# A four-layer graph-attention kernel: one layer summed by VectorE, sums taken two steps later, neighbour places in pairs

## The chip, the cores and the metric

The kernel runs on one core of a Trainium2 chip. The metric is the device time of one execution in microseconds; the number for a version is the median of its runs. A separate profiled execution gives the page and the trace, and its own time stands beside its span below.

The engines are named as in the profile: PE is TensorE (PEld its weight loads), DVE is VectorE, ACT is ScalarE, POOL is GpSimd, SP is SyncE. A line such as L753 is a line of the kernel before.

## The reference

There are 4096 nodes with 256 features each, in fp32, and a symmetric adjacency matrix in which each node has about eight neighbours on average, and itself. Four layers follow each other. Each takes the layer norm and ReLU of the features, applies one form of graph attention, and adds the result to the features:

```
h = relu(layernorm(x));  x = x + layer_l(h, adj)        # l = 0..3

layer 0:  Wh = h @ W            4 heads; e = leaky(s_i + s_j); softmax over neighbours; out = elu(sum_j a_ij Wh_j)
layer 1:  Wh = h @ W            1 head;  e = leaky(s1_i + s2_j); softmax;               out = Wh_i + sum_j a_ij h_j
layer 2:  Wh_head = h @ W_head + b   4 heads; the same kind of scores;                  out = sum_j a_ij Wh_j
layer 3:  q, k, v = h @ Wq + bq, ... 4 heads; scores q_i.k_j / 8, masked;               out = sum_j a_ij v_j
```

## The kernel before

The matrix is first read and turned into a list of neighbours for each node, and the nodes are sorted by how many neighbours they have. The 4096 sorted nodes then make 32 blocks of 128, one node in each partition. A block has as many places as its largest node has neighbours: `CAPS` goes from 23 down to 3 and sums to 277; 15 of the 32 counts are even and 17 odd. Layer 0 treats up to six of the neighbours ahead, so that it fetches `max(CAPS - 6, 0)` places, 93 in all.

A place is one neighbour for each of the block's 128 nodes. It is fetched by an indirect DMA on POOL (`fetch`, L529) from the layer's table of rows in DRAM into one slot of a ring in SBUF. The ring has 64 slots in layer 1, 69 in layer 2 and 36 in layer 3, where a row holds a key and a value. `fill(i)`, called at the start of step i, issues the fetches of blocks up to four ahead, as long as slots are free. `ORDER` takes the blocks alternately from the large and the small end (0, 31, 1, 30, and so on).

Every layer runs the same loop of 32 steps, one block a step, and every engine gets its instructions in the order in which the program is written (`tc.manual_schedule()`); nothing reorders them. One step i does this, with b the block of the step, c the one before it and d the one before that:

1. `fill(i)`: fetches on POOL.
2. `first(c)`: the first part of `settle` (only layer 0 has work there, two ACT instructions at L767 and L768).
3. `scores(b)`: DVE forms the attention scores of all places (in layer 3 with the products of queries and keys at L680 and L683), and ACT takes the exponential (L697) into `p`, a tile in PSUM.
4. `second(d)`: the norm's last part, ACT's ReLU (L507), PE's transposes (L515), ACT's copy of them (L516) and PE's product with the next layer's weights (L522, by `times` from `advance`).
5. `weigh(b)`: DVE normalises `p` (L732 to L734), multiplies the block's own row by its share (L741) and up to eight places at a time by theirs (L749). PE adds them up: one matmul with the identity for the own row (L745) and one for each place (L753), into the PSUM tile `acc`. An fp32 matmul appears in the trace as two passes, each with its weight load.
6. `settle(c)` goes on: DVE adds the sums of the previous block to the features (L780; L777 and L778 in layer 0; L772 in layer 3, which writes the output) and starts the statistics of the next norm.
7. `third(d)`: the rest of `advance`. It takes the product out of PSUM and makes the row of the next layer's table: L793 to L796 for layer 1, L800 and L801 for layer 2, L807 to L822 for layer 3. Rows for layers 2 and 3 are stored by SP's queue; those for layer 1 and the output by an indirect DMA on POOL (`send`, L535), which stands in POOL's order behind the fetches already issued.

After the loop the last two blocks are pushed through the remaining parts. The first fetch of a layer needs the whole table, and therefore the last row that the layer before it stores. PSUM holds two tiles for `acc`, three for `turned` and `times`, two for `p` and one for layer 3's query `q`.

Of the kernel before, what the change touches and what calls it, by code (L numbers as in the profile page):

```python
# [9 lines left out]
F32 = mybir.dt.float32  # L10
# [9 lines left out]
P = 128  # L20
# [45 lines left out]
class Sparse:  # L66
# [246 lines left out]
    def first_table(self, pool, rows, r):  # L313
# [8 lines left out]
        for k in range(4):  # L322
            t = 4 * r + k
            h = pool.tile([P, D], F32, name=f"s_h_t{t}", tag="h", bufs=2)
            nc.scalar.activation(
                h, xl[:, k, :], AF.Relu, bias=rn[:, 4 + k : 5 + k], scale=rn[:, k : k + 1]
            )
            ps = self.times(self.turned(pool, h, f"t0_{t}"), self.we0, W, f"t0_{t}")
            nc.scalar.copy(rows[:, t, :], ps)
# [180 lines left out]
    def turned(self, pool, h, name):  # L510
# [3 lines left out]
        for c in range(KC):  # L514
            nc.tensor.transpose(pt[:, ts(c, P)], h[:, ts(c, P)], self.ident)  # L515
        nc.scalar.copy(ht, pt[:, : KC * P].rearrange("p (c r) -> p c r", c=KC))  # L516
        return ht

# [26 lines left out]
    def layers(self):  # L545
        tc, nc, nt = self.tc, self.nc, self.nt
        with ExitStack() as ctx:
            big = ctx.enter_context(tc.tile_pool(name="s_big", bufs=1))
            self.pool = ctx.enter_context(tc.tile_pool(name="s_main", bufs=2))
            self.pacc = ctx.enter_context(tc.tile_pool(name="s_pacc", bufs=2, space=PSUM))  # L550
            self.pp = ctx.enter_context(tc.tile_pool(name="s_pp", bufs=3, space=PSUM))
            self.pe = ctx.enter_context(tc.tile_pool(name="s_pe", bufs=3, space=PSUM))

# [18 lines left out]
    def layer(self, l):  # L572

        nc, nt, vs = self.nc, self.nt, {}
# [6 lines left out]
        def fill(i):  # L584
            nonlocal at
            while todo and nt - len(todo) <= i + AHEAD:
                j = todo[0]
                K = self.slots(l, j)
                s = (at if at + K <= slots else 0) if K else 0
                if any(s < e and b < s + K for b, e in held.values()) or (l == 3 and len(held) > 3):  # L590
                    return
# [7 lines left out]
                for k in range(K):  # L599
                    at_k = self.near[:, j, k0 + k : k0 + k + 1]  # L600
                    self.fetch(ring[:, s + k, :], self.tab[l], at_k)
                held[j] = (s, s + K)
                at = s + K if K else at

        acc, behind, rows = {}, {}, {}

        def first(c):
            behind[c] = self.settle(l, c, acc.pop(c), made)
            next(behind[c])

        def second(d):
            if l < 3:
                ht = self.turned(self.pool, next(behind.pop(d)), f"{l + 1}_{d}")
                rows[d] = self.advance(l + 1, d, ht, made)
                next(rows[d])

        def third(d):
            if l < 3:
                next(rows.pop(d), None)
            for send in made:  # L620
                self.send(*send)
            made.clear()

        for i in range(nt):
            fill(i)
            b, c, d = (ORDER[k] if k >= 0 else None for k in (i, i - 1, i - 2))
            if c is not None:
                first(c)
            g = ring[:, held[b][0] : held[b][1], :]
            p = self.scores(l, b, self.rows[b], g)  # L630
            if d is not None:
                second(d)
            acc[b] = self.weigh(l, b, vs.pop(b) if l == 3 else self.rows[b][:, 0:D], g, p)
            del held[b]
            if c is not None:
                next(behind[c])
            if d is not None:
                third(d)
        c, d = ORDER[-1], ORDER[-2]
        first(c)  # L640
        next(behind[c])
        second(d)
        second(c)
        third(d)
        third(c)

    def scores(self, l, b, mine, g):
# [25 lines left out]
        else:  # L673
            q = self.pe.tile([P, D], F32, name=f"s_q_{b}", tag="q", bufs=1)
            nc.scalar.copy(q, mine[:, 0:D])
# [19 lines left out]
        )  # L695
        p = self.pe.tile([P, TOPK, H], F32, name=f"s_p_{l}_{b}", tag="p", bufs=2)
        nc.scalar.activation(p[:, : K + 1, :].rearrange("p k h -> p (k h)"), ek, AF.Exp)  # L697
# [17 lines left out]
    def weigh(self, l, b, me, g, p):  # L715
# [8 lines left out]
        else:  # L724
# [12 lines left out]
            mine = p[:, K, :]  # L737
        acc = self.pacc.tile([P, IB], F32, tag="acc", name=f"s_acc_{l}_{b}")
        v0 = 0 if l < 3 else D
        mev = pool.tile([P, D], F32, name=f"s_me_{l}_{b}", tag="me", bufs=2)  # L740
        nc.vector.tensor_tensor(  # L741
            mev.rearrange("p (h d) -> p h d", h=H), me.rearrange("p (h d) -> p h d", h=H),
            mine.unsqueeze(2).to_broadcast([P, H, D // H]), ALU.mult,
        )
        nc.tensor.matmul(acc[:, :D], lhsT=self.ident, rhs=mev, start=True, stop=(K == 0))  # L745
        for k0 in range(0, K, AT_ONCE):
# [4 lines left out]
            )  # L751
            for k in range(m):
                nc.tensor.matmul(  # L753
                    acc[:, :D], lhsT=self.ident, rhs=g[:, k0 + k, v0 : v0 + D],
                    start=False, stop=(k0 + k == K - 1),
                )
        return acc[:, :D]

    def settle(self, l, b, acc, made):
# [10 lines left out]
        if l == 3:  # L770
            y = pool.tile([P, D], F32, name=f"s_out_{b}", tag="out", bufs=3)
            nc.vector.tensor_tensor(y, xt, acc, ALU.add)  # L772
            made.append((self.out, self.own(b), y))
            yield None
            return
# [3 lines left out]
        else:  # L779
            nc.vector.tensor_tensor(xt, xt, acc, ALU.add)  # L780
        into = self.rows[b][:, 0:D] if l == 0 else None
# [607 lines left out]
```

## Time and profile before

| | us |
|---|---|
| median of 3 runs | 2269.25 |
| lowest, highest run | 2267.81, 2284.88 |
| profiled execution, its own time | 2277.38 |
| its span | 2275.6 |
| mean granted TensorE clock | 0.75 of full |
| DVE busy | 1270.9 (56% of the span) |
| POOL busy | 1212.4 (53%) |
| PE busy | 1175.5 (52%) |
| ACT busy | 444.1 (20%) |

| stretch, from a layer's first fetch to the next one's | from, to (us) | us |
|---|---|---|
| lists and sort | 0 to 522.46 | 522.5 |
| layer 0 | 522.46 to 813.45 | 291.0 |
| layer 1 | 813.45 to 1282.35 | 468.9 |
| layer 2 | 1282.35 to 1784.63 | 502.3 |
| layer 3 | 1784.63 to the end | 491.0 |

In a group's line of the page the columns are: line, engine, operation, tile written and tiles read, shape, count; then busy time in us and mean ns of one; then the engine's idle time just before these instructions, and what ended most of it. In the timeline they are start, busy time, engine, line, operation, and in brackets the idle time ahead of it and what released it. "remote" stands there where no releaser was found among this core's recorded events.

### The profile page before, as it was taken

What the parts mean: (1) busy time and instruction counts of PE and PEld (TensorE: products, weight loads), DVE (VectorE), ACT (ScalarE), POOL (GpSimd) and SP (SyncE); (2) the same over time, 40 slices, a digit from 0 to 9 for tenths busy, and PEclk for the clock granted to TensorE, in tenths of its full rate; (3) what the DMA queues carried; (4) which work ended last, traced back from release to release, by engine and by line L of the source; (5) the groups of instructions that cost most, each with busy time, mean ns of one, the idle gap of its engine ahead of it and who ended that gap; (6) DMA issues with size and microseconds to landing.
All of it is one profiled execution on the core that took longest, in us unless ns stands there. A gap on an engine that the chain in (4) does not pass through costs nothing. (4 is left out here: it accounts for less than half of the span.)

```text
span 2275.6 us, 17106 instructions
## 1 busy us (share of the span) xinstructions
PE 1175.5 (52%) x3977; PEld 795.2 (35%) x3999; DVE 1270.9 (56%) x3688; ACT 444.1 (20%) x1320; POOL 1212.4 (53%) x1354
## 2 busy tenths in 40 slices
PE   4767677611466613454566333566668242445354
PEld 2434334301344402333445222344446131334233
DVE  7657787711466711444466313455569465667666
ACT  5754343000233300111111101112123100000000
POOL 1055666556455457566653375655660465666662
PEclk9887889855687855677788756778789665667777
DMA  8988885305233244333432243333331555666662
GB/s 271 297 288 308 300 259 178 88 13 108 75 99 102 76 88 114 93 104 106 111 104 73 57 110 86 102 100 93 109 107 45 145 171 156 182 181 184 179 180 66
DMA packets 128244, 313.24 MB, mean 138 GB/s; under 512 B 31844, under 2 KB 58983, under 8 KB 128136
## 3 DMA queue, kind: packets, MB, share of 16 engines
q0 software_dynamic: 69088, 207.53, 33.3%
q1 hardware_dynamic: 59048, 104.55, 13.6%
q8 instruction: 34, 0.56, 0.1%
q14 instruction: 74, 0.61, 0.1%
HBM read 276.91 MB, written 35.07 MB: 137 GB/s over the span
## 5 line engine op out<-in xcount | busy, mean ns | idle before, releaser
L529 POOL DMA_INDIRECT s_ring<-s_tab,s_near x924 | 878.0, 950 | 599.5 <-issue 239.8
L753 PE MATMUL s_acc<-s_ring,s_ident 128*128 128x256 f32 x1848 | 510.0, 434 | 80.8 <-issue 59.9
L753 PEld LDWEIGHTS s_acc<-s_ring,s_ident 128*128 128x128 f32 x1848 | 409.6, 224 | 179.1 <-issue 73.6
L745 PE MATMUL s_acc<-s_me,s_ident 128*128 128x256 f32 x256 | 107.7, 511 | 410.6 <-issue 135.3
L749 DVE TENSOR_TENSOR s_ring<-s_ring,s_p 128x256 f32<-128x256 f32 (+7 forms) x169 | 267.1, 1605 | 0.0
L529 POOL DMA_INDIRECT s_g<-s_tab,s_listrow x192 | 184.2, 960 | 113.0 <-issue 53.9
L301 DVE MAX8 s_cand<-s_pt 128x8 f32<-128x256 f32 x512 | 188.4, 419 | 81.6 <-remote 40.5
L745 PEld LDWEIGHTS s_acc<-s_me,s_ident 128*128 128x128 f32 x256 | 61.7, 253 | 436.0 <-issue 232.8
L522 PE MATMUL s_ps<-s_we_l,s_ht 128*128 128x264 f32 x256 | 107.5, 560 | 129.7 <-ACT s_ht L516 92.2
L780 DVE TENSOR_TENSOR s_rx<-s_rx,s_acc 128x256 f32<-128x256 f32 x64 | 26.7, 418 | 246.5 <-remote 240.0
L697 ACT ACTIVATE s_p<-s_e 128x32 f32<-128x32 f32 (+13 forms) x119 | 23.1, 194 | 715.1 <-DVE s_e L693 252.5
L293 PE MATMUL s_pt<-s_low,s_mark 128*128 128x512 fp8e4 x256 | 110.2, 430 | 95.9 <-DVE s_cand L301 45.1
L286 ACT ACTIVATE s_low<-s_raw 128x1024 fp8e4<-128x1024 int32 x128 | 134.5, 1051 | 55.0 <-DMA s_raw<-in_adj_dram 45.1
L522 PE MATMUL s_ps_kv<-s_wkv,s_ht 128*128 128x512 f32 x128 | 88.5, 829 | 94.2 <-issue 69.3
L370 PE MATMUL s_ae<-s_g,s_ident 128*128 128x256 f32 x384 | 111.0, 449 | 19.8 <-issue 11.2
L522 PEld LDWEIGHTS s_ps<-s_we_l,s_ht 128*128 128x128 f32 x256 | 59.9, 259 | 156.2 <-ACT s_ht L516 104.3
L299 PE MATMUL s_pt<-s_places,s_stands 128*128 128x512 bf16 x235 | 100.9, 430 | 0.0
L370 PEld LDWEIGHTS s_ae<-s_g,s_ident 128*128 128x128 f32 x384 | 84.5, 226 | 45.2 <-issue 17.0
L680 DVE TENSOR_TENSOR s_ring<-s_ring,s_q 128x2048 f32<-128x2048 f32 (+7 forms) x48 | 81.0, 1687 | 25.5 <-DMA s_ring<-s_tab,s_near 25.2
L515 PE MATMUL s_pht<-s_ident,s_h 128*128 128x128 f32 x128 | 28.9, 310 | 127.9 <-issue 88.1
L386 ACT ACTIVATE s_y<-s_mv,s_eps 128x1 f32<-128x1 f32 x96 | 28.3, 295 | 312.8 <-DVE s_mv L383 130.9
L772 DVE TENSOR_TENSOR s_out<-s_rx,s_acc 128x256 f32<-128x256 f32 x32 | 13.4, 418 | 133.4 <-remote 99.6
(180 smaller groups left out, 1591.3 us busy)
## 6 DMA issues: line engine op xcount, KB each, us to landing
s_raw<-in_adj_dram SPq DMA_DIRECT2D x128, 512.0 KB
s_ring<-s_tab,s_near POOLq DMA_INDIRECT x924
s_tab<-s_kv SPq DMA_DIRECT2D x32, 256.0 KB
s_own<-s_to SPq DMA_DIRECT2D x32, 134.0 KB
s_tab<-s_rows SPq DMA_DIRECT2D x8, 528.0 KB
s_tab<-s_rx SPq DMA_DIRECT2D x32, 132.0 KB
s_xl<-in_x_dram SPq DMA_DIRECT2D x8, 512.0 KB
s_own<-s_xl SPq DMA_DIRECT2D x8, 512.0 KB
```

Source lines behind the costliest of these rows:

```text
L286: nc.scalar.activation(lo[:, ts(h, quarter)], raw, AF.Copy, saturate=False, accum_out=sums[:, r, h : h + 1],)
L293: nc.tensor.matmul(pt, lhsT=self.mark, rhs=lo[:, ts(g, IB)], start=True, stop=False)
L299: nc.tensor.matmul(pt, lhsT=stands[:, g, :], rhs=places, start=False, stop=True)
L301: nc.vector.max(out=cand[:, g * (IB // CH) + k, :], in_=pt[:, ts(k, CH)])
L370: nc.tensor.matmul(acc[:, :D], lhsT=self.ident, rhs=g[:, k, 0:D], start=False, stop=(k == E - 1))
L515: nc.tensor.transpose(pt[:, ts(c, P)], h[:, ts(c, P)], self.ident)
L522: self.nc.tensor.matmul(ps[:, :width], lhsT=ht[:, c, :], rhs=w[:, c, :], start=(c == 0), stop=(c == KC - 1),)
L529: self.nc.gpsimd.indirect_dma_start(out=out, out_offset=None, in_=table[:, :], in_offset=bass.IndirectOffsetOnAxis(ap=idx, axis=0),)
L680: nc.vector.tensor_tensor(kq, kq, q.unsqueeze(1).to_broadcast([P, m, D]), ALU.mult)
L745: nc.tensor.matmul(acc[:, :D], lhsT=self.ident, rhs=mev, start=True, stop=(K == 0))
L749: nc.vector.tensor_tensor(v, v, p[:, k0 : k0 + m, :].unsqueeze(3).to_broadcast([P, m, H, D // H]), ALU.mult)
L753: nc.tensor.matmul(acc[:, :D], lhsT=self.ident, rhs=g[:, k0 + k, v0 : v0 + D], start=False, stop=(k0 + k == K - 1),)
```

## The change

Four things are changed, all within the layers.

In layer 1, DVE forms the sum itself. The own row times its share is written to `acc` by one tensor_scalar, and each place is added by one scalar_tensor_tensor, which multiplies the row by its share and adds the result to `acc` in PSUM. The eight-place products and all of PE's sums are gone in that layer. The block is settled in the same step (S = 0), its norm and product follow one step later (N = 1), and `p` lies in SBUF.

In layers 0, 2 and 3, the sums of a block are used two steps later (S = 2) and the norm and product three steps later (N = 3), with four accumulator tiles instead of two. To make room for these, `p` (two slices in turn) and the query `q` of layer 3 share one bank of PSUM.

In all layers, taking up the product and sending or storing the row (`third`) comes one step after the product, behind the scores. The transposes and their copy are parted: `norm` issues the transposes early in the step, and `product` issues the copy and the product.

In layers 2 and 3, PE adds places in pairs: one matmul of 512 columns takes two places into the two halves of the accumulator, and DVE adds both halves when the block is settled. A block with an odd number of places has its own row in one more ring slot, as the partner of the last place. For an even number the own share is halved and a matmul reads the own row for both halves. A block takes an even number of ring slots for that.

```diff
-            self.pacc = ctx.enter_context(tc.tile_pool(name="s_pacc", bufs=2, space=PSUM))
+            self.pacc = ctx.enter_context(tc.tile_pool(name="s_pacc", bufs=4, space=PSUM))
+            shares = ctx.enter_context(tc.tile_pool(name="s_pe", bufs=1, space=PSUM))
...
-            self.pe = ctx.enter_context(tc.tile_pool(name="s_pe", bufs=3, space=PSUM))
+            self.turns = 0
+            self.shares = shares.tile([P, IB], F32, name="s_shares")
...
-                s = (at if at + K <= slots else 0) if K else 0
+                room = K + (K % 2 if l > 1 else 0)
+                s = (at if at + room <= slots else 0) if K else 0
...
+        S, N = (0, 1) if l == 1 else (2, 3)
         for i in range(nt):
             fill(i)
-            b, c, d = (ORDER[k] if k >= 0 else None for k in (i, i - 1, i - 2))
-            if c is not None:
-                first(c)
+            b, c, d, e = (ORDER[k] if k >= 0 else None for k in (i, i - S, i - N, i - N - 1))
+            if S:
+                settle(c, (0,))
+            norm(d)
             g = ring[:, held[b][0] : held[b][1], :]
-            p = self.scores(l, b, self.rows[b], g)
-            if d is not None:
-                second(d)
-            acc[b] = self.weigh(l, b, vs.pop(b) if l == 3 else self.rows[b][:, 0:D], g, p)
+            p = self.scores(l, b, self.rows[b], g[:, : self.slots(l, b), :])
+            third(e)
+            if S:
+                settle(c, (1,))
+            product(d)
+            sums[b] = self.weigh(l, b, vs.pop(b) if l == 3 else self.rows[b][:, 0:D], g, p)
             del held[b]
-            if c is not None:
-                next(behind[c])
-            if d is not None:
-                third(d)
+            if not S:
+                settle(b)
...
+            q = self.shares[:, IB - D :]
...
+        if l == 1:
+            p = pool.tile([P, TOPK, H], F32, name=f"s_p_{l}_{b}", tag="p", bufs=2)
+        else:
+            p = self.shares[:, ts(self.turns % 2, TOPK * H)].rearrange("p (k h) -> p k h", h=H)
...
+        both = self.pacc.tile([P, 2, D], F32, tag="acc", name=f"s_acc_{l}_{b}")
+        acc = both[:, 0, :]
+        self.turns += 1
+        if l == 1:
+            nc.vector.tensor_scalar(acc, me, p[:, K, :], None, ALU.mult)
+            for k in range(K):
+                nc.vector.scalar_tensor_tensor(
+                    acc, g[:, k, 0:D], p[:, k, :], acc, ALU.mult, ALU.add
+                )
+            return acc
...
+        if full:
+            nc.vector.tensor_scalar(mine, mine, 0.5, None, ALU.mult)
...
+        elif full:
+            nc.tensor.matmul(
+                both, lhsT=self.ident, rhs=mev.unsqueeze(1).to_broadcast([P, 2, D]),
+                start=True, stop=False,
+            )
...
+            for k in range(k0, k0 + m, 2 if pairs else 1):
+                if pairs:
+                    nc.tensor.matmul(
+                        both, lhsT=self.ident, rhs=g[:, k : k + 2, v0 : v0 + D],
+                        start=(k == 0 and not full), stop=(k + 2 >= K),
+                    )
...
-            nc.vector.tensor_tensor(y, xt, acc, ALU.add)
+            nc.vector.tensor_tensor(y, xt, acc[:, 0, :], ALU.add)
+            nc.vector.tensor_tensor(y, y, acc[:, 1, :], ALU.add)
...
-            nc.vector.tensor_tensor(xt, xt, acc, ALU.add)
+            for part in (acc[:, 0, :], acc[:, 1, :]) if l == 2 else (acc,):
+                nc.vector.tensor_tensor(xt, xt, part, ALU.add)
```

The functions `settle(c, parts)`, `norm`, `product` and `third` of the new loop:

```
def settle(c, parts=(0, 1)):
    if 0 in parts and c in sums:
        behind[c] = self.settle(l, c, sums.pop(c), made)
        next(behind[c])
    if 1 in parts and c in behind:
        next(behind[c])

def norm(d):
    if l < 3 and d in behind:
        turning[d] = self.turned(self.pool, next(behind.pop(d)), f"{l + 1}_{d}")
        next(turning[d])

def product(d):
    if d in turning:
        rows[d] = self.advance(l + 1, d, next(turning.pop(d)), made)
        next(rows[d])

def third(d):
    if d in rows:
        next(rows.pop(d), None)
    for send in made:
        self.send(*send)
    made.clear()
```

After the loop, the last three blocks of `ORDER` are pushed through these parts where S is 2, and the last one or two in layer 1.

## The prediction

> **What bounds the kernel now.** I read the page's groups first, then cut the layers into stretches, then opened one stretch engine by engine. From the groups of the page:
>
> ```profile
> L529 POOL DMA_INDIRECT s_ring<-s_tab,s_near x924 | 878.0, 950 | 599.5 <-issue 239.8
> L753 PE MATMUL s_acc<-s_ring,s_ident 128*128 128x256 f32 x1848 | 510.0, 434 | 80.8 <-issue 59.9
> L749 DVE TENSOR_TENSOR s_ring<-s_ring,s_p 128x256 f32<-128x256 f32 (+7 forms) x169 | 267.1, 1605 | 0.0
> L780 DVE TENSOR_TENSOR s_rx<-s_rx,s_acc 128x256 f32<-128x256 f32 x64 | 26.7, 418 | 246.5 <-remote 240.0
> ```
>
> L529 has 93 + 3 x 277 = 924 fetches. Undisturbed they start every 1.25 us (0.95 busy, 0.30 issue), so 277 need 347 us. L753 counts two passes for each fp32 matmul. L780's idle is the odd entry: DVE waits 240 us for sums of a PE that is half idle. The windows run from a layer's first fetch to its last, then to the next layer's first fetch (layers 1, 2, 3):
>
> ```profile
> core 0: us, PE busy (x) PEld busy (x) DVE busy (x) ACT busy (x) POOL busy (x), PEclk, DMA share, GB/s
> 813.45:1231.80 418.35, 189.24 (x654) 144.18 (x655) 181.82 (x616) 46.01 (x154) 262.71 (x277) 0.71 0.40 106
> 1231.80:1282.35 50.55, 39.22 (x157) 29.07 (x156) 37.98 (x141) 12.12 (x38) 0.01 (x1) 0.94 0.08 25
> 1282.35:1711.70 429.35, 217.13 (x712) 147.13 (x713) 196.92 (x570) 62.29 (x211) 263.13 (x277) 0.73 0.39 101
> 1711.70:1784.63 72.93, 60.80 (x231) 41.55 (x229) 60.41 (x183) 23.62 (x79) 0.00 (x0) 0.98 0.12 41
> 1784.63:2234.20 449.57, 185.63 (x555) 135.12 (x556) 276.38 (x373) 18.10 (x87) 290.14 (x304) 0.67 0.61 177
> 2234.20:2275.60 41.40, 21.38 (x65) 15.55 (x63) 25.75 (x34) 1.45 (x7) 4.96 (x6) 0.79 0.09 29
> ```
>
> While fetching no engine is full; with the fetches over, the same code runs well. Successive L741 in layer 1's tail start at 1236.52, 1243.62 and 1250.90: 7 us a step, against some 13 a step before. So the work of a step isn't the limit. The timeline from 853 us shows what is:
>
> ```profile
> 853.62 12.07 PE L753 MATMUL s_acc<-s_ring,s_ident 128*128 128x256 f32 x43 [0.98 <-issue]
> 862.46 0.16 DVE L733 RECIPROCAL s_t<-s_t 128x1 f32<-128x1 f32 x1 [1.06 <-issue]
> 863.86 0.17 DVE L734 TENSOR_TENSOR s_p<-s_p,s_t 128x4 f32<-128x4 f32 x1 [1.24 <-issue]
> 867.35 0.19 PEld L753 LDWEIGHTS s_acc<-s_ring,s_ident 128*128 128x128 f32 x1 [1.84 <-issue]
> 868.75 0.38 PE L753 MATMUL s_acc<-s_ring,s_ident 128*128 128x256 f32 x1 [2.42 <-issue]
> 893.95 0.58 PE L753 MATMUL s_acc<-s_ring,s_ident 128*128 128x256 f32 x1 [1.52 <-issue]
> 927.01 0.42 DVE L780 TENSOR_TENSOR s_rx<-s_rx,s_acc 128x256 f32<-128x256 f32 x1 [60.47 <-remote]
> ```
>
> PE issues 43 passes in 12 us; then PE and DVE start one instruction every 1.40 us, and from 894.5 to 927.0 no compute engine starts anything. POOL fetches on until its ring slots run out:
>
> ```profile
> 908.90 0.94 POOL L529 DMA_INDIRECT s_ring<-s_tab,s_near  x1 [1.72 <-remote]
> 914.50 0.94 POOL L529 DMA_INDIRECT s_ring<-s_tab,s_near  x1 [4.66 <-remote]
> ```
>
> Such stretches recur near 970, 1000, 1363, 1473, 1885, 1944 and 2105 us. They come when POOL fetches at full pace and PE runs dense 256-wide passes at full clock, one per 0.215 us with a weight load for each. There is none with POOL silent, none while DVE alone issues 5 instructions per us (847 to 857), none at half clock (0.427 us a pass, 1859 to 1865). I infer a limit on instructions or their completion signals, PE's mostly. It isn't shown: columns streamed would fit as well.
>
> [...]
>
> **The change, part by part.** Sums are made against the profiled execution: 2277.4 us, span 2275.6. The median is 8.1 lower.
>
> *Layer 1, DVE sums.* Gone are (277 + 32) x 2 = 618 passes and their loads, and the 8-place products, 80.7 us of DVE's 219.8. Added are 277 scalar_tensor_tensor of 128x256 into PSUM. The existing ones with PSUM operands start 0.46 us apart (586.31, 586.77, 587.23): 127.4 us. DVE has 219.8 - 80.7 + 127.4 = 266.5, or 8.3 us a step. Fetches give 277 x 1.253 / 32 = 10.85 a step, so the longer DVE step lies beside them. Settling moves into the same step, and the wait at L780 goes; late next is the fetch. The ring is freed by DVE: a block's slots wait for its last product, as they waited for PE. The tail becomes landing 3.1, scores 2.7, normalising 0.8, nine sums 4.1, statistics and norm 3.0, turn and product 2.7, add 0.4, store 2.6 = 19.4. Floor 347.1 + 19.4 = 366.5; now 418.35 + 50.55 = 468.9; lost 102.4. Of layer 1's 811 passes (654 + 157 in the windows) 193 stay, transposes and the next layer's products, or 24%, so I let about a fifth of the loss stay too: -80 (bounds -102 and 0, as the rivals have it).
>
> *Layer 2, pairs.* 618 passes of 256 columns become 162 matmuls or 324 passes of 512: 277 places, one own term for 17 odd blocks, and two halves for 15 even ones give 324 halves. With turns and products a step falls from (712 + 231) / 32 = 29 passes to 20, the sums' twice as long; their columns are the same within 5% (324 x 512 against 618 x 256 would be 618 x 268). DVE gains 32 more adds (14.4) and 15 halvings (about 0.2 each, near the small operations' 0.16): 257 + 17 = 274, 8.6 a step, beside the fetches. In the tail three blocks are drained where two were; the third costs 3.5 (1777.43 to 1780.96 between two such). From last L741 to next fetch is 22 now, so 22 + 3.5 + 5.7 for landing and scores = 31. Floor 347.1 + 31 = 378; now 502.3; lost 124. Half comes back: -62. Bounds 0 (columns count) and -124.
>
> *Layer 3, pairs.* The (555 + 65) / 32 = 19.4 passes a step become 10.2. Floor 304 POOL operations x 1.253 = 381, and 28 of tail: 409 against 491, lost 82. DVE's 302 has 17 added: 10 a step against 11.9. The rounded room in 36 slots leaves two blocks fetched ahead instead of three at some eight steps[...]. I take -50, between 0 and -82.
>
> *Layer 0 and the lag.* Passes are unchanged. Sums used two steps on with four accumulators let DVE's and ACT's elementwise work (L767, L777) meet sums long done. The later product takes its add, L793, and store past a whole step; each of its sends (L535 on POOL) now queues behind one more fill of fetches, where sends waited 73.5 us on ACT:
>
> ```profile
> POOL s_tab L535 <- ACT s_rx L795: 73.5, 12, 17.8
> DVE s_kv L807 <- PE s_ps_kv L522: 55.5, 16, 6.5
> ```
>
> The wait at L807 should go likewise; late next is the transpose. DVE queues the next products behind it. The longer drain costs 4 to 5 in layer 0 (the 3.5 of a third block and the add and send behind it). I take -15 for it (bounds -50 and +10), since waits hidden by fetches return nothing.
>
> Sum: -80 - 62 - 50 - 15 = -207; 2277.4 - 207 = 2070 as profiled, 2062 on the median.
>
> **Rivals.** *Columns, not instructions* (0.25): pairs halve instructions and keep columns, so layers 2 and 3 keep their stretches. For it: PE's load appears as columns and instructions alike. Against: DVE slows too. Gains 80 + 15 + about 20 from the lag = -115: 2155. *All stretches go* (0.11): each layer falls to its floor, -(102 + 124 + 82 + 25) = -333: 1936. For it: the tails. Against: layer 2 still makes 20 passes a step. *No change* (0.04): the cause lies in the fetches' own traffic, and a stretch only moves: 2269. *Slower* (0.10): the per-place chain of layer 1 is taken by the slow pace. Then a place costs 1.40 us instead of 0.46, since one instruction does what 1/8 did: 277 x 1.40 + 32 x 4.35 of other DVE work (266.5 - 127.4, by block) + 20 = 547 against 469, +78, with nothing gained elsewhere: 2347. For it: DVE ran at 1.24 to 1.40 us per instruction from 862 on. Against: PE's share of the load is away then. It decides from about 85 of the 277 at the slow pace, where 85 x 0.94 = 80 takes all that layer 1 gains.
>
> **How the numbers follow.** The forecast has 0.50: 2062. The range goes down to 1955, short of the 1936 case, and up to 2200, past the 2155 case[...]; the slow and no-change cases are outside. About one per cent is what a measurement can tell here (the three runs span 17 us). Faster by over 1% 0.86, within 1% 0.04, slower by over 1% 0.10.
>
> **What would show it.** Right: layer 1's window near 385 us, no L753 in it, L529 without gaps, sums 0.46 us apart, and fewer stretches at 1.40 us in layers 2 and 3; L780's wait for remote mostly gone. Wrong: layer 1's sums over 1 us apart; POOL's ring waits as long as before in layers 2 and 3 (then columns); tails well beyond 20 and 31 us; DVE waiting at L680 for its query.

## The result, and the profile after

The changed kernel takes 2241.39 us (2237.67 to 2246.91, four runs) where the kernel before takes 2274.45 in the same comparison: a ratio of 0.9866 (95% interval 0.983 to 0.9902), a gain of 1.3%. The forecast was 2062. Two later comparisons of the same pair, on two chips, gave 0.9924 (0.9902 to 0.9946) and 0.9986 (0.9965 to 1.0007). So the change is worth between 1.3% and nothing there. The sign that was forecast was measured in two of three comparisons; of the 207 us that were forecast, 33 came in the first.

The profiled execution took 2241.77 us (span 2240.0). Its layers, from first fetch to next first fetch, against the kernel before:

| | before | after | forecast of the difference | measured |
|---|---|---|---|---|
| layer 0 | 289.7 | 278.6 | -15 | -11.1 |
| layer 1 | 468.9 | 500.6 | -80 | +31.7 |
| layer 2 | 502.3 | 475.7 | -62 | -26.6 |
| layer 3 | 490.9 | 467.6 | -50 | -23.3 |

(The stage ahead of layer 0, which the change leaves alone, differs by 6 us between the two executions. Layer 0 is counted here from the first fetch of a place.)

The windows of the changed kernel, cut as before, for layers 1, 2 and 3 (microseconds of each engine, instructions in brackets):

```profile
core 0: us, PE busy (x) PEld busy (x) DVE busy (x) ACT busy (x) POOL busy (x), PEclk, DMA share, GB/s
796.10:1224.80 428.70, 70.38 (x150) 36.55 (x150) 230.07 (x786) 42.00 (x152) 261.66 (x276) 0.50 0.38 102
1224.80:1296.70 71.90, 19.70 (x42) 10.21 (x42) 56.77 (x199) 11.44 (x40) 0.96 (x2) 0.50 0.06 20
1296.70:1697.80 401.10, 209.42 (x487) 100.29 (x488) 211.42 (x616) 61.12 (x210) 262.45 (x277) 0.77 0.40 107
1697.80:1772.40 74.60, 58.83 (x161) 28.72 (x160) 61.96 (x183) 22.90 (x80) 0.94 (x1) 0.98 0.13 44
1772.40:2204.40 432.00, 195.43 (x301) 74.14 (x300) 297.42 (x424) 21.17 (x90) 287.11 (x302) 0.69 0.62 183
2204.40:2240.00 35.60, 17.20 (x27) 6.10 (x25) 19.68 (x30) 0.91 (x4) 7.79 (x8) 0.71 0.14 46
```

PE's instructions in layer 1 fell from 811 to 192, as the change says, and yet the layer's fetches take 428.7 us instead of 418.35, and its tail 71.9 instead of 50.55. The groups of the page show that the operations are those that were expected, too:

```profile
L531 POOL DMA_INDIRECT s_ring<-s_tab,s_near x924 | 877.3, 949 | 613.3 <-issue 301.1
L806 PE MATMUL s_acc<-s_ring,s_ident 128*128 128x512 f32 x588 | 321.4, 701 | 209.8 <-issue 103.9
L772 DVE SCALAR_TENSOR_TENSOR s_acc<-s_ring,s_p,s_acc 128x256 f32<-128x256 f32 x277 | 135.7, 490 | 22.4 <-DVE s_acc L772 10.0
```

Here is the beginning of layer 1, where PE is still silent:

```profile
833.72 5.21 DVE L772 SCALAR_TENSOR_TENSOR s_acc<-s_ring,s_p,s_acc 128x256 f32<-128x256 f32 x10
840.53 0.49 DVE L772 SCALAR_TENSOR_TENSOR s_acc<-s_ring,s_p,s_acc 128x256 f32<-128x256 f32 x1 [0.90 <-DVE s_acc L772]
841.94 0.49 DVE L772 SCALAR_TENSOR_TENSOR s_acc<-s_ring,s_p,s_acc 128x256 f32<-128x256 f32 x1 [0.92 <-DVE s_acc L772]
857.33 0.42 DVE L840 TENSOR_TENSOR s_rx<-s_rx,s_acc 128x256 f32<-128x256 f32 x1 [0.90 <-DVE s_acc L772]
869.89 0.69 PE L516 MATMUL s_pht<-s_ident,s_h 128*128 128x128 f32 x2 [78.13 <-issue]
```

Ten sums go at 0.52 us each, and then DVE starts one instruction every 1.40 us, the pace that the kernel before showed, although PE issues nothing in the 78 us ahead of 869.89. So the slow pace needs no dense passes. In layer 2 the old picture is still there, with fewer passes. The first pair of lines is the same place in the kernel before, the second is the change:

```profile
1319.01 1.22 PE L745 MATMUL s_acc<-s_me,s_ident 128*128 128x256 f32 x2 [39.87 <-issue]
1396.79 0.42 DVE L780 TENSOR_TENSOR s_rx<-s_rx,s_acc 128x256 f32<-128x256 f32 x1 [68.53 <-remote]
```

```profile
1335.20 14.06 PE L806 MATMUL s_acc<-s_ring,s_ident 128*128 128x512 f32 x28 [41.72 <-DVE s_ring L801]
1376.48 0.88 DVE L840 TENSOR_TENSOR s_rx<-s_rx,s_acc 128x256 f32<-128x256 f32 x2 [26.27 <-remote]
```

PE's 28 passes for two blocks end by 1349.3, but DVE uses the sums of the first only at 1376.48, 41.3 us after the first pass. That block has 24 passes: 1.7 us each. In the kernel before it was 1396.79 - 1319.01 = 77.8 us for the same block with 48 passes, 1.6 us each. Half the instructions make the stretch shorter by about half; they don't remove it. What comes late here is the news of finished work, a semaphore update on which the next engine waits. The trace has updates of PE's semaphore at 1354.06, 1359.66, 1365.26 and 1376.46, when PE's last pass is up to 27 us old, and DVE starts 0.02 us after the last of them.

Layer 1's tail shows how long DVE's own step is. It is read from L770 to L770:

```profile
1231.68 0.49 DVE L770 TENSOR_SCALAR s_acc<-s_rx,s_p 128x256 f32<-128x256 f32 x1
1242.10 0.49 DVE L770 TENSOR_SCALAR s_acc<-s_rx,s_p 128x256 f32<-128x256 f32 x1
1252.14 0.49 DVE L770 TENSOR_SCALAR s_acc<-s_rx,s_p 128x256 f32<-128x256 f32 x1
```

A step with nothing in its way takes 10.0 to 10.4 us with eight or nine places; it took 7.0 to 7.3 before, and 8.3 in the prediction's sum.

### The profile page after: what moved, and what is told of

It is laid out like the page before. It is cut to its first block, busy times and chain, and to the rows that moved or that the text cites. A ratio compares the mean times of both kernels' runs of the same rounds, so it can differ in the third digit from the quotient of the medians.

```text
span 2240.0 us, 14984 instructions
## 1 busy us (share of the span) xinstructions
PE 1026.8 (46%) x2793; PEld 538.4 (24%) x2793; DVE 1366.8 (61%) x4011; ACT 436.8 (19%) x1320; POOL 1211.9 (54%) x1354
## 4 chain that ended last, share of the span: by engine, by line
DVE 38%; PE 15%; issue 15%; another core or an unknown queue 11%; POOL 8%; DMA 7%; ACT 3%; ACTq 1%; SPq 0%; DVEq 0%; POOLq 0%
DVE s_acc L772 7%; POOL s_ring L531 5%; PE s_acc L806 4%; DVE s_ring L801 4%; PE s_ae L371 3%; PE s_ps_kv L524 2%; DMA s_raw<-in_adj_dram 2%; DVE s_cand L301 2%; DVE s_ring L705 2%; DMA s_ring<-s_tab,s_near 2%; DVE s_e L708 2%; DVE s_st L383 2%; DVE s_rx L840 1%; POOL s_lists L446 1%
## 5 line engine op out<-in xcount | busy, mean ns | idle before, releaser
L806 PE MATMUL s_acc<-s_ring,s_ident 128*128 128x512 f32 x588 | 321.4, 701 | 209.8 <-issue 103.9
L806 PEld LDWEIGHTS s_acc<-s_ring,s_ident 128*128 128x128 f32 x588 | 131.2, 230 | 396.8 <-issue 272.8
L524 PE MATMUL s_ps<-s_we_l,s_ht 128*128 128x264 f32 x256 | 115.1, 594 | 158.3 <-ACT s_ht L518 111.6
L801 DVE TENSOR_TENSOR s_ring<-s_ring,s_shares 128x2048 f32<-128x2048 f32 (+7 forms) x121 | 187.4, 1572 | 0.0
L516 PE MATMUL s_pht<-s_ident,s_h 128*128 128x128 f32 x128 | 34.2, 360 | 316.8 <-issue 220.0
L772 DVE SCALAR_TENSOR_TENSOR s_acc<-s_ring,s_p,s_acc 128x256 f32<-128x256 f32 x277 | 135.7, 490 | 22.4 <-DVE s_acc L772 10.0
L705 DVE TENSOR_TENSOR s_ring<-s_ring,s_shares 128x2048 f32<-128x2048 f32 (+7 forms) x48 | 81.1, 1690 | 53.4 <-DMA s_ring<-s_tab,s_near 33.3
L299 PE MATMUL s_pt<-s_places,s_stands 128*128 128x512 bf16 x256 | 109.5, 428 | 0.0
L516 PEld LDWEIGHTS s_pht<-s_ident,s_h 128*128 128x128 f32 x128 | 18.2, 172 | 356.7 <-issue 247.5
L725 ACT ACTIVATE s_shares<-s_e 128x32 f32<-128x32 f32 (+8 forms) x87 | 17.4, 200 | 416.9 <-DVE s_e L718 136.0
L794 PE MATMUL s_acc<-s_me,s_ident 128*128 128x512 f32 x60 | 42.1, 792 | 107.9 <-issue 34.5
L686 DVE TENSOR_TENSOR s_e<-s_ring,s_rx 128x8 f32<-128x8 f32 (+12 forms) x87 | 15.8, 182 | 117.9 <-DMA s_ring<-s_tab,s_near 110.5
```

What stands on the lines that cost most here:

```text
L299: nc.tensor.matmul(pt, lhsT=stands[:, g, :], rhs=places, start=False, stop=True)
L524: self.nc.tensor.matmul(ps[:, :width], lhsT=ht[:, c, :], rhs=w[:, c, :], start=(c == 0), stop=(c == KC - 1),)
L705: nc.vector.tensor_tensor(kq, kq, q.unsqueeze(1).to_broadcast([P, m, D]), ALU.mult)
L772: nc.vector.scalar_tensor_tensor(acc, g[:, k, 0:D], p[:, k, :], acc, ALU.mult, ALU.add)
L801: nc.vector.tensor_tensor(v, v, p[:, k0 : k0 + m, :].unsqueeze(3).to_broadcast([P, m, H, D // H]), ALU.mult)
L806: nc.tensor.matmul(both, lhsT=self.ident, rhs=g[:, k : k + 2, v0 : v0 + D], start=(k == 0 and not full), stop=(k + 2 >= K),)
```

## The experiments

The runs fell on several chips. On all but one of them the kernel before takes about 2275 us; on one it takes 1937.94. Each ratio is to the kernel before on the same chip, and runs on different chips are compared by these ratios; layers are compared on one chip or, where said, between runs whose other layers agree.

**Layer 1 back on PE.** In the change, `S, N = (2, 3)` for layer 1 too, and its two branches for `l == 1` taken out:

```diff
-        S, N = (0, 1) if l == 1 else (2, 3)
+        S, N = (2, 3)
...
-        if l == 1:
-            nc.vector.tensor_scalar(acc, me, p[:, K, :], None, ALU.mult)
...
```

> The change with layer 1 alone put back: products of eight places on DVE, one matmul a place on PE, sums used two steps later as in the other layers. Layer 1 took 468.9 us before and 500.6 after. Theory A (the DVE chain is what cost time in layer 1: 10.0 us a step undisturbed instead of 7, and one instruction every 1.40 us in the slow stretch): layer 1 falls to 450 to 470 us and the whole to about 2200 to 2215. Rival (the chain is harmless, layer 1 was slowed by the new order of its steps or by where its stretch happened to fall): layer 1 stays at 490 to 510, the whole within 10 us of 2241.

It took 2239.69 us, 0.9841 (0.9796 to 0.9886). Layer 1 took 477.0 us, 24 below the change's 500.6. The whole did not follow (forecast 2200 to 2215): layer 2 ran the same code and took 490.1 instead of 475.7. Layers vary by this much between chips and executions, so a part of the change is better read from pairs of runs on one chip. On this chip the next run has the change's layer 1, and takes 508.2 us for it, so that DVE's chain costs 31 us there.

**Pairs off.** One matmul a place again in layers 2 and 3; the extra ring slot and the second add at settling go with it:

```diff
-                room = K + (K % 2 if l > 1 else 0)
+                room = K
...
-        pairs = l > 1
+        pairs = False
...
```

> The change with one matmul of 256 columns a place again in layers 2 and 3 (and no extra ring slot, no halved share, one add at settling); all else as changed. If PE's instructions set the length of the slow stretches, layers 2 and 3 (475.7 and 467.6 us) go back most of the way to 502 and 491, the whole to 2275 to 2295. If columns or the fetches set it, they stay within 10 us each and the whole within 2230 to 2255.

It took 2295.30 us, 1.0076 (1.0047 to 1.0104), 1 to 2% above the change's ratios, as it should be if PE's instructions set the stretches' length. But the size is less than the total says. A later run of the change itself had the same layers 0 and 1 as this one (286.7 and 509.7 against 287.5 and 508.2), and beside that one layer 2 is 501.6 against 490.6 and layer 3 473.2 against 470.0. Pairs are worth 11 us in layer 2 and 3 in layer 3 there. Two runs with pairs on the chip of this one agree: 490.1 and 468.7 us with layer 1 on PE, 488.5 and 468.8 with the two chains below.

**Two chains instead of one.** Layer 1's sums alternate between the two halves of the accumulator:

```diff
-                nc.vector.scalar_tensor_tensor(
-                    acc, g[:, k, 0:D], p[:, k, :], acc, ALU.mult, ALU.add
-                )
-            return acc
+                half = both[:, (k + 1) % 2, :]
+                if k == 0:
+                    nc.vector.tensor_scalar(half, g[:, k, 0:D], p[:, k, :], None, ALU.mult)
+                else:
+                    nc.vector.scalar_tensor_tensor(
+                        half, g[:, k, 0:D], p[:, k, :], half, ALU.mult, ALU.add
+                    )
+            return both
...
```

> The change with layer 1's DVE chain split into two that alternate (own row and odd places in one half of the accumulator, even places in the other, both halves added at settling), so that no instruction needs the one just before it. If the 1.40 us of the slow stretch is the delay until an instruction's completion is seen by the next one that needs it, sums there start about 0.7 us apart, the first stretch of layer 1 shortens by 15 to 25 us and the whole by 10 to 25. If it is a rate at which each engine may issue, they stay 1.40 apart, and the 32 extra adds make it 5 to 15 us slower.

Both halves are added at settling. It took 2277.87 us, 1.0020 (0.9999 to 1.0041), and layer 1 took 513.3 us, 5 more than with one chain on the same chip (508.2 with pairs off). The slow stretch looks as it did:

```profile
857.77 0.49 DVE L776 SCALAR_TENSOR_TENSOR s_acc<-s_ring,s_p,s_acc 128x256 f32<-128x256 f32 x1 [0.91 <-DVE s_acc L776]
859.17 0.49 DVE L776 SCALAR_TENSOR_TENSOR s_acc<-s_ring,s_p,s_acc 128x256 f32<-128x256 f32 x1 [0.92 <-issue]
860.57 0.49 DVE L776 SCALAR_TENSOR_TENSOR s_acc<-s_ring,s_p,s_acc 128x256 f32<-128x256 f32 x1 [0.91 <-DVE s_acc L776]
```

The steps of 1.40 us stayed. That speaks for a rate at which each engine gets on, but doesn't settle it: the brackets still name DVE's own last sums as what was waited for, so the edit may not have freed each sum of the one before it.

**Fetches at a slower pace.** A memset on POOL after every fetch of a place, with no use but its time:

```diff
+            self.idle = big.tile([P, 128], F32, name="s_idle")
...
                     self.fetch(ring[:, s + k, :], self.tab[l], at_k)
+                    nc.gpsimd.memset(self.idle, 0.0)
```

With 128 elements a partition:

> The change with one memset of 128x128 on POOL after every fetch of a place, in all four layers, so that fetches start some 1.45 to 1.6 us apart instead of 1.25. Theory F (fetches at full pace are what slows every other engine's instructions to one in 1.40 us): no stretch of that pace is left, layer 1 becomes bound by fetches or DVE at about 435, layer 2 about 450, layer 3 about 475 to 490, the whole 2150 to 2190. Rival (the stretches come from the compute engines' own bursts): the stretches stay and slower fetching adds to them: 2270 to 2330.

It took 2242.62 us, 0.9843 (0.9802 to 0.9885). Fetches started 1.335 us apart. The expected time was missed, but the picture changed:

```profile
852.57 0.49 DVE L774 SCALAR_TENSOR_TENSOR s_acc<-s_ring,s_p,s_acc 128x256 f32<-128x256 f32 x1 [0.58 <-DVE s_acc L774]
853.27 0.49 DVE L774 SCALAR_TENSOR_TENSOR s_acc<-s_ring,s_p,s_acc 128x256 f32<-128x256 f32 x1 [0.21 <-DVE s_acc L774]
854.66 0.49 DVE L774 SCALAR_TENSOR_TENSOR s_acc<-s_ring,s_p,s_acc 128x256 f32<-128x256 f32 x1 [0.91 <-DVE s_acc L774]
```

Steps of 0.70 and 1.40 us are mixed, and layer 1 took 481.8 us although its fetches were slower. With 256 elements, on the chip where the kernel before takes 1937.94 us:

> The change with a memset of 128x256 on POOL after every fetch of a place: some 1.47 us from fetch to fetch, where the memset of 128x128 gave 1.335 and left a pace of 0.70 and 1.40 us in the slow stretches. Theory F (the fetches' pace sets the stretches): the 0.70 and 1.40 us steps are gone, DVE's chain in layer 1 runs at 0.52 throughout, layer 1 falls below 460 and the whole to 2130 to 2210. Rival (the stretches shrink only by as much as fetching gets slower): layer 1 stays at 475 to 490, the whole at 2235 to 2260.

It took 2089.07 us there, 1.0775 (1.0716 to 1.0833). That is below the range that theory F gave, but slower than the kernel before on that chip. The time of the kernel before there, 331 us below the 2269 of the first profile, is about the sum of what the prediction had counted as lost (333). No trace of an unpaced kernel was taken on that chip, so that its layers have no slow stretches is inferred. The stage ahead of the layers is in favour of it. The median gap of its 192 fetches is 1.25 us in every run (141 of 191 gaps are 1.25 or 1.26 in the first profile of the kernel before). On the chips of 2275 us PE, DVE and ACT together wait 72 to 96 us there for "remote", which is how late news of finished work shows in the profile: in layers 1 and 2 of the kernel before, the 33 waits of over 4 us at L780 and L516 all end 0.02 us after an update of PE's semaphore. On the chip of 1938 us they don't wait for it once, there or in any layer of the four paced kernels run on it.

A still longer memset, of 416 elements, on the same chip:

> The same with a memset of 128x416: some 1.6 us from fetch to fetch, 443 us for 277. Theory F: no slow stretch at all, every layer bound by its fetches: about 465 in layer 1, 475 in layer 2, 505 in layer 3, the whole some 30 us above the run with 1.47. Rival: slow stretches are seen at this pace too, and the whole is above 2290.

2207.30 us, 1.1386 (1.1323 to 1.145), with 1.573 us from fetch to fetch: layers of 457.5, 472.7 and 515.7 us, all bound by fetches and without a slow step, but 118 us above the run with 256 elements, not 30.

The same pace on a chip where the kernel before takes 2274.62 us, beside the unpaced change:

> The changed kernel as it is, once more. The calls so far ran on two chips: on one the kernel before takes about 2275 us and every engine falls to one instruction in 1.40 us while POOL fetches at full pace; on the other it takes about 1938. Where the kernel before takes 2275, the ratio should repeat 0.987. Where it takes 1938, there are no such stretches to win back: theory, layer 1 is then bound by DVE's chain (37 us to the first block, 32 x 10.1, 14 to the end: 374 us) and the layers with pairs by their fetches, so the change is worth -10 to +25 us; rival (the lag and the pairs gain by themselves, whatever the chip), 30 to 60 us faster.

> The change with the memset of 128x256 after every fetch, run beside the unpaced one. On the chip with slow stretches: theory F (the fetches' pace sets them), layer 1 below 460 us and the whole 90 to 150 us below the unpaced change; rival, within 20 us of it. On the chip without them it can only lose: it was at 2089 there.

The change alone: 2249.49 us, 0.9924. With the memset: 2114.75 us, 0.9354 (0.9296 to 0.9411). An instruction that does nothing takes 135 us off, more than the whole change. These are the windows of layers 1 and 2 of the paced run, then its fetches, then the beginning of its layer 1:

```profile
core 0: us, PE busy (x) PEld busy (x) DVE busy (x) ACT busy (x) POOL busy (x), PEclk, DMA share, GB/s
776.10:1177.40 401.30, 84.44 (x180) 43.87 (x180) 277.61 (x944) 52.16 (x183) 352.89 (x553) 0.50 0.43 111
1177.40:1197.20 19.80, 5.63 (x12) 2.93 (x12) 10.15 (x40) 3.00 (x10) 1.32 (x3) 0.50 0.12 35
1197.20:1598.90 401.70, 247.81 (x580) 118.46 (x581) 251.62 (x733) 73.24 (x253) 353.50 (x553) 0.81 0.42 111
1598.90:1632.20 33.30, 25.25 (x68) 12.87 (x67) 21.89 (x67) 10.72 (x37) 1.24 (x2) 0.91 0.17 57
```

```profile
777.06 0.32 POOL L610 MEMSET s_idle<- 128x256 f32 x1
777.54 0.97 POOL L531 DMA_INDIRECT s_ring<-s_tab,s_near  x1 [0.16 <-issue]
778.51 0.33 POOL L610 MEMSET s_idle<- 128x256 f32 x1
779.00 0.95 POOL L531 DMA_INDIRECT s_ring<-s_tab,s_near  x1 [0.16 <-issue]
```

```profile
817.21 12.04 DVE L774 SCALAR_TENSOR_TENSOR s_acc<-s_ring,s_p,s_acc 128x256 f32<-128x256 f32 x23
834.54 1.54 DVE L774 SCALAR_TENSOR_TENSOR s_acc<-s_ring,s_p,s_acc 128x256 f32<-128x256 f32 x3
842.34 7.31 DVE L774 SCALAR_TENSOR_TENSOR s_acc<-s_ring,s_p,s_acc 128x256 f32<-128x256 f32 x14
```

All 23 sums of the first block run without a break. Fetches start 1.44 us apart and never wait, so layer 1 ends 19.8 us after its last fetch: the tail that the prediction worked out as 19.4. Layer 2's tail is 33.3 against 31. With 192 elements instead (1.389 us apart), on a third chip:

> The change with a memset of 128x192 after every fetch: about 1.38 to 1.39 us from fetch to fetch. If the limit is near 1.40, the pace seen in the stretches, some slow steps of 0.70 us are left and layers 1 and 2 take about as long as with 1.44 (421 and 435). If 1.38 is past the limit, they fall by 277 x 0.05 = 14 us each and the whole to about 2070 to 2090 where the kernel before takes 2275.

2219.62 us, 0.9737 (0.9676 to 0.9799): slow steps of 0.70 and 1.40 us are back, and layers 1 and 2 take 474.5 and 479.8 us, where with 256 elements they take 422.7 and 436.7 on the same chip (in a run below); neither case of the expectation has that. For the changed kernel the limit lies between 1.389 and 1.44 us a fetch. The pace was changed by memsets alone; fetches spaced in another way were not run.

**What the change is worth with paced fetches.** The kernel before with the same memset, first on the chip of 1938 us and then on one of 2275:

> The kernel before with the memset of 128x256 after every fetch and nothing else. Theory F: its stretches go as well, POOL's fetch of the next block no longer waits on a delayed PE, layers 1 and 2 fall from 469 and 502 to 430 to 450 each, the whole to 2160 to 2220 from about 2275. Rival (before, the stretches came from PE's dense passes, which stay): 2270 to 2310.

> The kernel before with the memset of 128x256 after every fetch, on a chip where the kernel before takes 2275 us if the call falls on one. If the stretches alone separate the two kernels, it comes within 1% of the paced change (0.935 of the kernel before): 2110 to 2135 us. If the change gains much by itself, it is above 2160.

On the first: 2108.06 us, 1.0884 (1.0819 to 1.0948), against 1.0775 for the paced change; less than expected, since that chip is faster unpaced. On the second: 2178.62 us, 0.9578 (0.9543 to 0.9613), against 0.9354 for the paced change on another chip of that kind. By the expectation that is the case in which the change gains much by itself. Layers 1 and 2 took 441.4 and 455.8 us, 19 each above the change at this pace on the same chip (422.7 and 436.7), all of it behind the last fetch:

```profile
1187.80:1227.40 39.60, 29.82 (x108) 22.36 (x108) 23.89 (x91) 8.68 (x27) 1.30 (x3) 0.80 0.09 28
1629.60:1683.10 53.50, 44.20 (x162) 29.48 (x160) 40.15 (x121) 16.56 (x56) 1.28 (x2) 0.95 0.13 46
```

But this is no comparison without slow stretches. At 1.44 us a fetch the kernel before still gets news of finished work late on this chip. These are waits of its layer 1 (total, times, longest):

```profile
ACT s_ht L516 <- remote: 149.3, 19, 10.7
DVE s_rx L782 <- remote: 79.5, 18, 7.6
```

Together that is nearly as much as without the memset (236 us in the first profile). In layer 2 it is 150 us. On the same chip, at the same pace, there is none in layer 1 of the change, with 192 PE instructions, nor with pairs there, with 516; here PE has 810. In layer 2 these two, with about 647, wait 13 and 19 us, and the kernel before has 941. So the pace that is slow enough seems to go with the number of PE's instructions as well; the kernels differ in the order of their steps too, so that this isn't shown. On the chip of 1938 us, where neither kernel waits in this way, the kernel before has tails of 24.6 and 28.4 us instead of 39.6 and 53.5. With paced fetches the change brings about 2% on the chips of 2275 us, and 0.9% on that one (2089.07 against 2108.06).

**Which part brings what.** On the chip of the paced run, the lag alone (no pairs, layer 1 on PE), and pairs in layer 1 too:

> The change without pairs and with layer 1 on PE: only the order of the steps (sums two steps on, product three, taken up one step later), the four accumulators and the shared bank are left. If the gain in layer 3 (490.9 to 467.6 us) is the lag's, it is here too (within 8 us); if it is the pairs', layer 3 goes back to above 483. Whole: 2250 to 2275 where the kernel before takes 2275.

> The change with layer 1 on PE in pairs. With slow stretches: layer 1 goes from 500 us to 445 to 470, since pairs gained about 19 in layer 2 and PE sums 24 here; the whole to 2190 to 2220. Without them: layer 1 is bound by fetches, 5 to 25 us below the DVE chain.

The lag alone took 2246.92 us, 0.9899 (0.9874 to 0.9924), as fast as the whole change beside it (2249.49). Layer 3 took 466.5 us, so that gain is the lag's. Layer 2 took 513.3 against the change's 477.4, so pairs gain 36 us there; layer 1 took 476.2 against 500.0, so DVE's chain gives 24 of them back. The lag itself doesn't shorten these two layers; in the first profile of the kernel before they took 468.9 and 502.3. With pairs on PE in layer 1 the kernel took 2212.48 us, 0.9785 (0.9707 to 0.9862), and layer 1 467.4.

Under paced fetches this order disappears:

> The change with layer 1 summed by PE in pairs like layers 2 and 3 (lag of two steps, both halves added at settling), and the memset of 128x256 after every fetch. If the DVE chain still costs anything once fetches are paced, layer 1 is 10 to 30 us shorter than in the run with the memset alone; if fetches bind, it is within 8 us of it.

> Layer 1 on PE in pairs, and the memset of 128x256 after the fetches of layers 0 to 2 only; layer 3 fetches at full pace, where pacing has gained nothing (482 us paced, 470 unpaced). Layer 3 goes back to 465 to 472, layers 1 and 2 are fetch-bound at about 425 and 437: the whole 2095 to 2110 where the kernel before takes 2275.

> The change as it is, with the memset of 128x256 in layers 0 to 2 only. As in the run beside it for layer 3; if the DVE chain is as good as pairs on PE once fetches are paced, it is within 8 us of that run.

On the chip of 1938 us, pairs in layer 1 took 2098.53 us (1.0819) against 2089.07 for the chain, and layer 1 427.0 against 421.1. With layer 3 left unpaced, on a chip of 2275, they took 2123.06 us (0.9333, 0.9290 to 0.9375), and the chain 2119.66 (0.9323, 0.9284 to 0.9362). Layer 3 took 468.7 and 468.5, as expected, but the whole missed the 2095 to 2110 that was expected. These two and the change with all layers paced (0.9354) are the fastest versions on chips of 2275 us, and their intervals overlap.

**The change a third time.** The same pair on one more chip:

> The changed kernel as it is. If the kernel before takes about 1938 us in this call (a chip without the slow stretches), layers 1 and 2 gain what they gain under paced fetches, about 19 us each, less what DVE's longer steps cost when fetches come every 1.25 us: 1900 to 1950. If it takes about 2275, the ratio is between 0.984 and 0.994 as in the two comparisons so far.

The kernel before took 2278.21 us on that chip, and the change 2275.86, 0.9986 (0.9965 to 1.0007): outside the expected interval. Its layer 1 took 509.7 us and its layer 2 490.6. The change without pacing has not been timed on the chip of 1938 us.

## Why the prediction was wrong

*The cause of the slow stretches* is the step that failed first. The prediction took them for a limit on instructions "or their completion signals, PE's mostly", and so expected layer 1 to be rid of four fifths of its loss (-80) when 76% of PE's instructions went. It got 31.7 us longer. The runs show that DVE alone falls to one instruction in 1.40 us while POOL fetches every 1.25 us and PE is silent, and that the pace of the fetches takes layer 1 of the change from 500.0 us to 421.1 on one chip; at 1.335 and 1.389 us the slow steps are mixed with shorter ones, at 1.44 there are none. Two parts of the prediction's picture hold: what comes late is the news of finished work, and PE's instructions do count, as pairs show in layer 2 and as the kernel before at 1.44 us suggests. But layer 1 hardly needed them. The prediction had named "DVE slows too" as an argument against the rival with columns, and did not ask what it meant for the forecast. It had also dismissed the fetches' own traffic as a case of 0.04.

*The rival that ended slower* described layer 1's sign and mechanism: the chain did fall to 1.40 us a sum. Its price was not right: it needed 85 sums at that pace, and only 14 are seen in layer 1 (and small instructions around them), yet the layer lost 31.7 us. By the runs beside it, 24 to 31 us of that go with the chain.

*DVE's step is the term that was mis-sized.* It was put at 8.3 us from a busy time of 266.5. The busy time came to 286.8, or 9.0 a step. A sum takes 0.52 us from start to start, not 0.46: of the three instructions that it was priced from, the one at 586.77 alone reads PSUM, and none writes it, while the sums do (490 ns against 421 for L840). The gaps between instructions and the waits for ACT were left out. At 10.0 to 10.4 us DVE is hardly faster than the fetches (10.85 a step) and makes up little of a delay. And the slow beat goes on delaying it: from 932.3 to 1232.2 us 23 steps take 13.0 each, ten of them 14.7 to 17.5, with waits such as this for its own result:

```profile
1130.71 0.33 DVE L733 TENSOR_SCALAR s_eq<-s_ring,s_own_f 128x230 bf16<-128x230 f32 x1
1135.85 0.39 DVE L737 TENSOR_REDUCE s_has<-s_eq 128x10 f32<-128x230 bf16 x1 [4.80 <-remote]
```

After the first stretch a block's sums start some 75 to 95 us behind its last fetch, and still do 20 blocks later; the ring is full, POOL waits (14.81 us in the line below), and the backlog is paid in a tail of 71.9 us where 19.4 was forecast. How much of it is the longer step and how much the beat was not separated; with fetches at 1.44 us the same chain leaves a tail of 19.8. The kernel before caught up at 7 us a step.

```profile
905.14 0.95 POOL L531 DMA_INDIRECT s_ring<-s_tab,s_near  x1 [0.30 <-issue]
920.90 0.95 POOL L531 DMA_INDIRECT s_ring<-s_tab,s_near  x1 [14.81 <-issue]
```

*Pairs* had the right direction in layer 2 (-26.6 of -62). They gained 11 to 36 us there by comparisons on like runs. In layer 3 their share is 3 us or nothing: the -23.3 is the lag's, which the forecast's sum has only in layer 0. What the shared bank and the shorter look-ahead cost was not measured apart; layer 3 as a whole is faster (467.6 against 490.9 us) and its tail shorter (35.6 against 41.4 us).

*Layer 0 and the lag* had the right sign and, in the first profile, the right size: -11.1 for -15. The two later profiles of the change have -12.8 and -3.0.

*The tails in the floors* were right. Once the fetches are paced, 19.8 and 33.3 us stand for the 19.4 and 31 of the sum.

What stays open is what POOL's fetches and the other engines' instructions share, and why one chip takes 331 us less for the same program. The runs show a pace at which it sets in, not the thing itself. One rival is untested, a part of the profiler's recording in it. Every run on record has a span and a granted clock from the chip's own records, so none can be taken as unrecorded. And the chips differ in just this: in the paced change's trace from the chip of 1938 us all of DVE's semaphore updates are recorded (3514, for 3513 instructions that make one), in that from a chip of 2275 us 2725, and in the first trace of the change, also from such a chip, 2346.

## What to carry to other kernels

When engines that have nothing to do with each other fall into the same slow beat, look for what runs beside all of them and change its pace before moving work from one engine to another: here a useless memset after each fetch was worth 6.0% on the changed kernel (2114.75 against 2249.49) and 4.2% on the one before, and the whole rewrite 0 to 1.3%. It has to be measured on the chip that matters, since on another the memset cost the kernel before 8.8%. And when work moves to another engine, read the step from start to start in an undisturbed stretch with all its gaps, and compare that with the supplier's pace; a step just under it makes up little of a delay (here 10.0 to 10.4 us against 10.85, at most 0.85 us a step).

## What the runs showed of the hardware

- On the chips of 2275 us, while indirect fetches of 128 rows start every 1.25 us, DVE and PE can each be held to one instruction in 1.40 us (PE with its weight loads from 869 to 887 us in the kernel before, DVE from 840.53 to 857.33 us in the change). In the changed kernel steps of 0.70 and 1.40 are mixed at 1.335 and 1.389 us a fetch, and there are none in layers 1 and 2 at 1.44. The fetches themselves keep their pace until they wait for ring slots: 1.25 us apart up to 906 us in the kernel before and up to 905 us in the change.
- On those chips the news of finished work comes late: in layer 2 of the change PE's semaphore was updated up to 27 us after its last pass, and DVE started 0.02 us after that. In the kernel before, with 810 PE instructions in layer 1, ACT and DVE still waited 228.8 us for such news at 1.44 us a fetch; with 516 and 192, in the change with and without pairs there, there was no such wait.
- In layer 1 of the change a scalar_tensor_tensor of 128x256 in fp32 that writes PSUM took 490 ns and a tensor_scalar 487, where a tensor_tensor that reads PSUM and writes SBUF took 421.
- The same program took 1937.94 us on one chip and about 2275 on four others.
